# An adaLN block with a gated delta rule and a mixture of experts: the loads of x in the periods issued on ScalarE's queue instead of SyncE's

## Chip, cores and metric

The kernel runs on one core of a Trainium2 chip. The metric is the device time of one execution in microseconds (us); lower is better. A core has TensorE (PE, matmuls), VectorE (DVE), ScalarE (ACT), GpSimd (POOL) and SyncE (SP, which only issues transfers here). SP and ACT both can issue DMAs through a queue of their own. In the profile, "SPq L423" is an issue on SP's queue from line 423, and "ACTq L423" one on ACT's.

## Reference

The input x has 4 batches of 1024 tokens with 256 channels. From a condition c come six vectors for each batch: shift, scale and gate for the attention (sa, ca, ga) and for the feed-forward part (sb, cb, gb).

```python
h = _layernorm(x) * (1 + ca) + sa
x = x + ga * attention(h)
h = _layernorm(x) * (1 + cb) + sb
x = x + gb * moe(h)
```

The attention has 16 heads of 64. q, k and v are projections of h, each followed by a causal convolution over 4 tokens and a silu; k is normalised. Then a state S of 64 x 64 for each head goes from token to token:

```python
upd = vt - at[..., None] * (S @ kt)
S = clip(at * S + bt * outer(upd, kt), -5.0, 5.0)
ot = S @ qt
```

The outputs are multiplied by silu(h Wg + bg) and projected by Wo. The mixture of experts sends each token to the best 2 of 8 experts, each 256 to 512 to 256 with a gelu between, and adds the two results by their softmax weights.

## The kernel before, in words

The attention is computed in chunks of 32 tokens: one chunk is 4 batches x 32 tokens = 128 rows, and there are 32 chunks. Two neighbouring chunks make a pair; there are 16 pairs. Inside a chunk the recurrence is solved as a triangular system. `adaln_block` (L182) calls `chunks` (L362), which does the attention and the routing, and then `blocks` (L2149), which computes the experts in blocks of 256 gathered rows.

The main loop (L1505) has 16 periods. Period g runs the two state passes of pair g (stream c) and at the same time prepares pair g+1: its rows, routes, decays, keys and queries, values, triangle, rows of k and scaled keys. The order in which the steps of these streams are written is the string PLAN (L59): each letter takes one step of the stream that it names, in `work` (L1350). The letter x, twice in the string, is a step of `loads` (L1391), which loads one chunk of x; period g loads chunks 2g+6 and 2g+7, so chunks 6 to 31 are loaded in periods 0 to 12. The chunks before are loaded at the start (L446 and `later_loads`).

One chunk's load (`load_x`, L417) takes one of 9 buffers named x and issues 8 DMAs in `fill_x` (L423), 16 KB each. The rows loaded are first read in the next period, by the layer norm's statistics (L489) and by ACT (L509). Much later POOL adds the attention's result in place (L1278), SP stores the sum to x_scratch (L1280) and from there to out (L1283); then the buffer is free.

The order of the instructions on PE, DVE, ACT and POOL is the order in which the program writes them. SP's order is left to a scheduler, which places SP's issues by their dependences. The change touches L1393 alone. What the prediction follows, in the order of a period:

- L900, on SP: the decays of the pair go to g_scratch. L994, on SP: they come back spread over the partitions as sc. POOL multiplies kq by sc (L1001) and copies the last column (L1004).
- L586, on POOL: an indirect DMA sends routed rows. L1231, on POOL: aS, the decayed state, which needs L1004's result. L1196, on DVE: S = ps_s + aS.
- L920 to L956, on DVE: the triangular system, among it X (L943) and prod (L948), both with two inputs in SBUF.
- L619, on ACT: the first tap of the convolution out of PSUM for q, k (kq) and v; L628, on DVE, the other taps; L634, on ACT, silu. The projections on PE are L610, those of the gate L780 (ACT reads them in L787).
- L1149 on PE and L1154 on ACT: u, the updates of a chunk, copied out of PSUM in two halves; L1167 and L1208 on PE and L1218 on ACT: the outputs o; L1187 on PE: what u adds to the state.
- L853 on PE and L864 on ACT: kk and kk_r, the products of keys of the next pair; L1019 on PE: ps_t.
- L433 and L436, on SP: the weights w_v and w_gt; L428: w_kq. L1338, on SP: clearing of rows_scratch.

Of the kernel before, what the change touches and what calls it, by code (L numbers as in the profile page):

```python
# [361 lines left out]
def chunks(ctx, tc, a, nch, con, ones, modt, modc, x1_dram, rt, out):  # L362

    nc = tc.nc
# [18 lines left out]
    def take(pool, shape, name, tag=None, bufs=1, **more):  # L383
        tag = tag or name
        assert is_open.get(tag, 0) < bufs, tag
        is_open[tag] = is_open.get(tag, 0) + 1
        if bufs > 1:
            more["bufs"] = bufs
        return pool.tile(shape, F32, name=name, tag=tag, **more)
# [27 lines left out]
    def load_x(c, eng=nc.sync):  # L417
        x_of[c] = take(s3, [P, D], "x", bufs=9)
        fill_x(c, x_of[c], eng)

    def fill_x(c, x, eng):
        for there, here in by_batch(a["x"][c], x):
            eng.dma_start(here, there)  # L423
# [966 lines left out]

    def loads(first):  # L1391
        for c in range(first, min(first + 2, nch)):
            load_x(c)  # L1393
            yield

    def both_of(pair, prev):
# [108 lines left out]
    for g in range(npair):  # L1505

        prev, passes, bounds = both_of(now, prev)
        streams = dict(l=now.below(), c=passes, b=bounds, x=loads(2 * g + 6), z=clears())
        after, finished[:] = list(finished), []
        if g + 1 < npair:  # L1510
            x = newer
            newer = [x_of.pop(2 * g + 4 + par) for par in range(2)] if g + 2 < npair else None
            now = Pair(g + 1, x, newer, after)
            streams.update(preparing(now))
            work(streams, PLAN)
        else:

            sending = sent(after, nch - 2)
            for name in LAST:
                next(sending if name == "m" else streams[name], None)  # L1520
            work(streams, "")
# [885 lines left out]
```

## Time and profile before

| | us |
|---|---|
| three runs | 1906.1, 1913.18, 1915.0 |
| their median | 1913.18 |
| the profiled execution, its own time | 1922.9 |
| its span, from the first to the last instruction | 1921.1 |
| granted TensorE clock, mean | 0.919 |
| PE busy | 1632.0 |
| DVE busy | 1482.3 |
| ACT busy | 826.7 |
| POOL busy | 716.4 |
| one middle period (620.52 to 711.67 us): PE, DVE, ACT, POOL busy | 81.41, 75.68, 44.71, 36.88 |

The busy times are of one execution under the profiler. Issues of DMAs are not counted as busy; they are shown on rows of their own (SPq, ACTq). In a row of the timeline, the first number is the start from the beginning of the span, the second the time that it lasted, both in us; "x2" joins two neighbours of one kind; square brackets hold the idle time of the engine just before, and what ended it. The chain follows the work that ended last back from the end, at each step to what released it. An engine may have much idle time in all and yet set the end in one stage, so what follows reads one period closely.

### The profile page before, as it was taken

To read this page: it belongs to the slowest core of one execution; us is meant where nothing else is said; L and a number is where in the kernel's file an instruction comes from. 1 tells how busy PE (TensorE), PEld (TensorE's weight loads), DVE (VectorE), ACT (ScalarE), POOL (GpSimd) and SP (SyncE) were. 2 spreads that over 40 slices of the span, in tenths; PEclk is the share of its full clock that TensorE was granted. 3 is DMA by queue.
4 is the path that set the end of the run, shared out by engine and by line. 5 is a ranking of instruction groups with operands and counts; after the bars stand their busy time and mean duration, and the time that the engine had idled before them with its cause. 6 is when DMAs were issued, how large, how long until landed. Compare 5 with 4: busy or idle time off the path is not lost.

```text
span 1921.1 us, 88201 instructions
## 1 busy us (share of the span) xinstructions
PE 1632.0 (85%) x38610; PEld 1297.1 (68%) x38610; DVE 1482.3 (77%) x3622; ACT 826.7 (43%) x1652; POOL 716.4 (37%) x913
## 2 busy tenths in 40 slices
PE   5578999889989898989898989898888675989994
PEld 3456676667676766767676767676667564878883
DVE  4678797968788888878787978797968335789973
ACT  3344545444545544545445444554443112334331
POOL 1032343424342525252534343433424432454343
PEclk9889998989999998989899989998989677999997
DMA  4455444443545445354535453636343216788882
GB/s 117 127 161 129 105 108 94 107 109 95 148 115 141 123 120 137 107 134 111 146 103 150 106 153 97 161 94 153 110 112 112 56 36 207 187 208 219 231 231 35
DMA packets 431490, 249.52 MB, mean 130 GB/s; under 512 B 242996, under 2 KB 410808, under 8 KB 430840
## 3 DMA queue, kind: packets, MB, share of 16 engines
q1 hardware_dynamic: 416488, 223.65, 43.6%
q0 software_dynamic: 13664, 18.38, 5.2%
q8 instruction: 306, 5.01, 1.1%
q10 hardware_dynamic: 944, 1.77, 0.3%
q14 instruction: 88, 0.72, 0.1%
HBM read 165.99 MB, written 81.87 MB: 129 GB/s over the span
## 4 chain that ended last, share of the span: by engine, by line
PE 66%; DVE 11%; issue 7%; POOL 5%; SPq 5%; DMA 4%; ACT 3%; POOLq 0%; DVEq 0%; ACTq 0%
PE ps_q L610 22%; PE ps_hm L2116 6%; PE ps_yb L2129 6%; PE ps_w L1265 5%; PE ps_gt L780 4%; PE ps_u L1149 3%; PE ps_kk L853 3%; PE ps_o L1208 2%; PE ps_z L1127 2%; SPq L423 2%; PE ps_t L1031 2%; PE ps_s L1187 2%; DMA sc<-g_scratch 2%; PE ps_t L1019 2%; DVE kq L628 2%
## 5 line engine op out<-in xcount | busy, mean ns | idle before, releaser
L628 DVE SCALAR_TENSOR_TENSOR kq<-ps_q,w_conv,kq 128x256 f32<-128x256 f32 x768 | 319.7, 476 | 150.2 <-ACT kq L619 149.6
L610 PE MATMUL ps_q<-hT,w_kq 128*128 128x280 f32 x1024 | 323.2, 460 | 58.9 <-issue 20.6
L610 PEld LDWEIGHTS ps_q<-hT,w_kq 128*128 128x128 f32 x1024 | 203.5, 213 | 125.9 <-issue 58.2
L619 ACT ACTIVATE kq<-ps_q,w_conv 128x256 f32<-128x256 f32 x256 | 142.4, 563 | 234.8 <-PE ps_q L610 233.1
L1001 POOL TENSOR_TENSOR kq<-kq,sc 128x512 f32<-128x512 f32 x128 | 163.5, 1299 | 143.6 <-DMA sc<-g_scratch 116.5
L2136 POOL DMA_INDIRECT out<-yb,at_b x72 | 120.4, 1672 | 190.2 <-DVE gate L2106 48.7
L628 DVE SCALAR_TENSOR_TENSOR v<-ps_q,w_conv,v 128x256 f32<-128x256 f32 x384 | 158.9, 476 | 41.9 <-ACT v L619 41.7
L1231 POOL TENSOR_TENSOR aS<-S,last 128x1024 f32<-128x1024 f32 x64 | 122.5, 1914 | 135.9 <-DVE S L1196 133.4
L780 PE MATMUL ps_gt<-hT,w_gt 128*128 128x256 f32 x512 | 144.3, 410 | 29.6 <-issue 20.5
L787 ACT ACTIVATE gate<-ps_gt,b_gt 128x256 f32<-128x256 f32 x128 | 60.5, 473 | 239.3 <-PE ps_gt L780 239.1
L610 PE MATMUL ps_q<-hT,w_v 128*128 128x280 f32 x512 | 153.5, 441 | 11.6 <-issue 4.7
L2116 PE MATMUL ps_hm<-hT,w 128*128 128x256 f32 x576 | 136.4, 392 | 7.6 <-issue 5.9
L2123 ACT ACTIVATE hm<-ps_hm,b 128x256 f32<-128x256 f32 x144 | 68.2, 474 | 167.5 <-issue 120.4
L2129 PE MATMUL ps_yb<-w,hm 128*128 128x256 f32 x576 | 130.3, 379 | 0.0
L2116 PEld LDWEIGHTS ps_hm<-hT,w 128*128 128x128 f32 x576 | 112.7, 197 | 25.9 <-issue 8.9
L610 PEld LDWEIGHTS ps_q<-hT,w_v 128*128 128x128 f32 x512 | 97.7, 204 | 47.3 <-issue 13.1
L780 PEld LDWEIGHTS ps_gt<-hT,w_gt 128*128 128x128 f32 x512 | 92.0, 194 | 53.1 <-issue 28.5
L1265 PE MATMUL ps_w<-w_o,yT 128*128 128x256 f32 x512 | 121.0, 391 | 4.3 <-DVE yT L1252 2.8
L1278 POOL TENSOR_TENSOR x<-x,add 128x256 f32<-128x256 f32 x32 | 29.0, 905 | 236.4 <-DVE add L1276 232.3
L2129 PEld LDWEIGHTS ps_yb<-w,hm 128*128 128x128 f32 x576 | 106.7, 190 | 13.4 <-DVE yb L2134 0.3
L1265 PEld LDWEIGHTS ps_w<-w_o,yT 128*128 128x128 f32 x512 | 98.2, 195 | 20.1 <-DVE yT L1252 3.0
L619 ACT ACTIVATE v<-ps_q,w_conv 128x256 f32<-128x256 f32 x128 | 71.3, 573 | 93.7 <-PE ps_q L610 93.7
(265 smaller groups left out, 3230.5 us busy)
## 6 DMA issues: line engine op xcount, KB each, us to landing
w<-in_w SPq DMA_DIRECT2D x72, 512.0 KB
rows_scratch<-zero_row SPq DMA_DIRECT2D x272, 132.0 KB
w_kq<-in_w_qkv SPq DMA_DIRECT2D x260, 128.0 KB
sc<-g_scratch SPq DMA_DIRECT2D x128, 256.0 KB
w_v<-in_w_qkv SPq DMA_DIRECT2D x130, 128.0 KB
w_gt<-in_w_g SPq DMA_DIRECT2D x260, 64.0 KB
u_scratch<-u SPq DMA_DIRECT2D x128, 128.0 KB
hb<-rows_scratch SPq DMA_DIRECT2D x36, 264.0 KB
```

The source lines that it names most:

```text
L610: nc.tensor.matmul(ps.rearrange("p y t -> p (y t)"), lhsT=w[:, dc], rhs=h_t[:, dc].rearrange("p x b t -> p (x b t)"), start=(dc == 0), sto ...
L619: nc.scalar.activation(o, ps[:, :, 0:TC], AF.Identity, scale=taps[:, 0:1], bias=taps[:, KC : KC + 1])
L628: nc.vector.scalar_tensor_tensor(o, ps[:, :, j : j + TC], taps[:, j : j + 1], o, op0=ALU.mult, op1=ALU.add)
L780: nc.tensor.matmul(ps, lhsT=wg[:, dc], rhs=self.h_t[:, dc, :, :, KC - 1 :].rearrange("p x b t -> p (x b) t"), start=(dc == 0), stop=(dc == 1),
L787: nc.scalar.activation(gate[:, hp].rearrange("p x b t -> p (x b t)"), ps.rearrange("p y t -> p (y t)"), AF.Silu, bias=b_gt[:, hp : hp + 1],)
L1001: nc.gpsimd.tensor_tensor(o, o, sc[:, h4 : h4 + 4], ALU.mult)
L1231: nc.gpsimd.tensor_tensor(aS.rearrange("q b h i -> q (b h) i"), S[:, bs].rearrange("q b h i -> q (b h) i"), self.pair.last[self.par][:, bs ...
L1265: nc.tensor.matmul(ps_w, lhsT=self.yT[:, hp].rearrange("q b t -> q (b t)"), rhs=w_o[:, hp], start=(hp == 0), stop=(hp == HP - 1),)
L2116: nc.tensor.matmul(ps, lhsT=self.w1[:, dc, fc * P : (fc + 1) * P], rhs=self.hT[:, dc], start=(dc == 0), stop=(dc == 1),)
L2123: nc.scalar.activation(self.hm[:, fc], ps, AF.Gelu, bias=self.b1[:, fc : fc + 1])
L2129: nc.tensor.matmul(ps, lhsT=self.hm[:, fc, s * P : (s + 1) * P], rhs=self.w2[:, fc], start=(fc == 0), stop=(fc == 3),)
L2136: return nc.gpsimd.indirect_dma_start(out=places, out_offset=bass.IndirectOffsetOnAxis(ap=self.at[:, s : s + 1], axis=0), in_=y, in_offset ...
```

## The change

The loads of `loads` are issued on ACT's queue. The number of DMAs, their sizes and their buffers stay the same, and so does the place in the plan.

```diff
     def loads(first):
         for c in range(first, min(first + 2, nch)):
-            load_x(c)
+            load_x(c, nc.scalar)
             yield
```

`load_x(c, eng)` passes the engine on to `fill_x`, which calls `eng.dma_start` for each of the 8 parts. ACT's order is the program's, so the 8 issues stand in ACT's stream where the letter x stands in the plan: the first block of a period between L619 of a v and L1218 of an o, the second between L619 of a v and L1154, the first half of u. SP's issues of the same period are placed anew by the scheduler.

## The prediction

> **What bounds the kernel now.** I read the busy shares and the chain that ended last on the page, then the chain inside one middle period, then each engine's timeline at the two places where the change puts work.
>
> ```profile
> PE 1632.0 (85%) x38610; PEld 1297.1 (68%) x38610; DVE 1482.3 (77%) x3622; ACT 826.7 (43%) x1652; POOL 716.4 (37%) x913
> ...
> PE 66%; DVE 11%; issue 7%; POOL 5%; SPq 5%; DMA 4%; ACT 3%; POOLq 0%; DVEq 0%; ACTq 0%
> ```
>
> PE is the body of the chain. The queue of SP holds 5% of it, and line 423, the loads of x, 2% of the span (about 40 us). The chain of waits from 632 to 658 us shows where these stand; its columns are start, us, what:
>
> ```profile
> 638.78 0.59 SPq L423
> ...
> 642.91 0.43 SPq L423
> ...
> 643.92 4.59 DMA sc<-g_scratch
> ...
> 648.68 3.24 POOL kq L1001 x2
> ...
> 654.68 1.89 POOL aS L1231
> ...
> 656.59 1.22 DVE S L1196
> ```
>
> The reader is to see eight loads of x ahead of the load of sc (L994), which POOL needs for kq, then for aS, which DVE adds into the state S. But how much of it binds? DVE's timeline says:
>
> ```profile
> 656.59 1.22 DVE L1196 TENSOR_TENSOR S<-ps_s,aS 128x1024 f32<-128x1024 f32 x1 [0.92 <-POOL aS L1231]
> ```
>
> DVE was busy up to 655.66 and then waited 0.92 us. The chain follows the last releaser, so 4.6 us of issues on it are worth 0.92 us; DVE's own work comes next. Over the whole run S waits 15.4 us for aS, 10 times.
>
> I count a period from its first store to g_scratch (L900), called t0: 632.37 us here. Periods are 91.3 us long (first kk_r to first kk_r: 711.67 less 620.52 is 91.15), but two are 99.9 (339.46 to 439.38, and 1353.53 to 1453.45).
>
> **The change part by part.** Chunks 6 to 31 move: 26 blocks of 8 DMAs, two blocks in each of 13 periods. PE, DVE and POOL keep their order; ACT gets block 1 after the second v (L619) before an o (L1218), block 2 after the second v before the first u (L1154). SP's other issues are put in a new order.
>
> *Removed from SP.* From 638.78 to 643.34 is 4.56 us per period before sc, and the same again elsewhere: SP is idle before L900, from 715 to 723.9, so nothing is gained there. SP then goes from L900 over two w_v and two clearing stores (L1338) to sc: sc leaves at about t0+5.8 instead of t0+11.0. The period without loads shows this: L900 at 1365.40, sc at 1371.17, kq on POOL at 1376.19, or t0+10.8; here it is t0+16.3. Gain: at most the wait of S, 0.92 per period, 15.4 in all. The weights that now go ahead of L900 lie in SP's 8.9 idle us; if those were gone, their issue (0.55 to 0.6 each) would delay L900.
>
> *Block 1 on ACT* (in the model period at 703.7, after the v at 703.15). An issue lasts 0.42 us and the gap to the next 0.045:
>
> ```profile
> L423 SPq DMA_DIRECT2D x<-in_x x248: 310/419/2070, 1.7 to 1285.1; - x124
> L423 ACTq DMA_DIRECT2D x<-in_x x8: 317/432/608, 1.4 to 7.6; - x8
> ```
>
> Eight on ACT are 8 x 0.477 = 3.8 us. If ACT ran them strictly between its computations, the o due at 704.26 would begin at 707.5. What is queued behind: o, two kq (L619), o, hT, two silu, and then kk_r at 711.67, which had 1.45 us of idle time before it. Following that string, kq comes 1.4 us late for DVE and PE, at 13 periods 18 us. If the issues run ahead while ACT waits for PE (it idles 0.78 us before that v, 0.54 before o, 0.92 before kq), the cost is 0. No row of before shows an issue between computations, as ACT's only issues stand ahead of its first one. So 0 to 18; I take 4, nearer to nothing, since the idle times just ahead add up to 2.2 us and the loads' own waits are for transfers long landed.
>
> [...]
>
> *Block 2 on ACT.* This is the place that costs:
>
> ```profile
> 634.05 0.56 ACT L619 ACTIVATE v<-ps_q,w_conv 128x256 f32<-128x256 f32 x1 [0.38 <-PE ps_q L610]
> 635.11 0.59 ACT L1154 COPY u<-ps_u 128x512 f32<-128x512 f32 x1 [0.49 <-PE ps_u L1149]
> 636.00 0.59 ACT L1154 COPY u<-ps_u 128x512 f32<-128x512 f32 x1 [0.31 <-PE ps_u L1149]
> 641.78 0.47 ACT L787 ACTIVATE gate<-ps_gt,b_gt 128x256 f32<-128x256 f32 x1 [5.20 <-PE ps_gt L780]
> ```
>
> Eight semaphores mark the landing of all these DMAs in turn, for both queues, so each issue waits for the transfer eight before it. Block 2's loads follow directly on SP's L900, w_v and L1338 and wait for their landing. A landing takes 3.0 us by the row nearest (x_scratch stored at 693.18, read from 696.14). The second L1338 leaves at about t0+3.9 and lands at t0+6.9; the load behind it and the last one follow, so the block ends at t0+7.7 to 8.9. The first u then ends at t0+8.3 to 9.5, instead of 635.70, t0+3.3. ACT is idle for 5.20 us after the two u, so ACT has room; PE has not: ps_o (L1167) starts at 639.51, t0+7.1, in the buffer that u frees. It comes 1.2 to 2.4 us late, the first S on DVE 0.3 to 1.5 late, ps_t (L1019) as much as ps_o. Against the gain of 0.92 on the second S that leaves +0.25 to +1.45 per period, 3 to 19 in all; I take the middle, 0.8, 13 x 0.8 = 10.
>
> *What the earlier sc meets.* In each of the five periods whose sc is early today (L900 at 171.83, 264.92, 351.37, 1365.40, 1465.62), at least one two-input DVE operation next to POOL's kq is 0.9 us too long: prod (L948) takes 1.91 to 2.00 instead of 1.04. Regular periods have none. I add 0.9 for the ten that become early: 9.
>
> Sum: 10 + 4 + 9 = 23 us.
>
> **Rivals.**
>
> *Collision of POOL and DVE.* The long periods are two of those with an early sc. Timeline of POOL and then DVE in the first:
>
> ```profile
> 367.35 0.97 POOL L586 DMA_INDIRECT rows_scratch<-row_h,at  x1 [0.21 <-issue]
> ...
> 368.37 1.91 POOL L1231 TENSOR_TENSOR aS<-S,last 128x1024 f32<-128x1024 f32 x1
> ...
> 370.52 2.47 POOL L1001 TENSOR_TENSOR kq<-kq,sc 128x512 f32<-128x512 f32 x2
> ```
> ```profile
> 362.26 1.93 DVE L948 TENSOR_TENSOR prod<-T,X 128x512 f32<-128x512 f32 x1
> ...
> 368.17 4.91 DVE L943 TENSOR_TENSOR X<-X,rk 128x64 f32<-128x64 f32 x1
> ```
> ```profile
> 376.91 2.04 PE L780 MATMUL ps_gt<-hT,w_gt 128*128 128x256 f32 x4 [5.15 <-issue]
> ```
>
> X (L943) takes 0.22 us elsewhere; here it lasts until POOL's string ends, and PE idles 5.15 us behind it. The other long period has 4.92 and 5.19. With SP relieved, all ten regular periods get the order of that second one. Price per period: 5.2 (PE's idle time) to 8.6 (99.9 less 91.3), together 52 to 86. It decides if X begins at t0+16.8 to 17.1, as aS begins. Against it: the late u moves DVE too, and where X began 1.2 us after aS (period of 1465.62) it lasted only 1.09.
>
> [...]
>
> *Hidden anyway.* Both blocks run ahead in ACT's idle time, landings are quick, u is as early as needed, and an 0.9 stall cancels the gain on S: within 0.5%, 1903.6 to 1922.7.
>
> *Faster.* If L1338 lands in 1.5 us or so, u is out by t0+6.5, before PE's ps_o; then the 15.4 us of S go, and the 4.7 of the first long period with them if its alignment shifts (L943 4.91 less 0.22): -10 to -20, 1893 to 1903.
>
> *It does not do what it says:* SP could keep waiting for the same landings, as the eight semaphores are shared; then sc leaves as late as now and only ACT's cost stays, +4 to +18. I count this within the forecast.
>
> **How the numbers follow.** The profiled execution took 1922.9 us (span 1921.1 and 1.8 around it), 0.5% above the median of the runs, 1913.2. 1922.9 + 23 = 1945.9, or 1936 on the scale of the median. The forecast's own range is 1925 to 1959 (the three terms at their ends: 3 + 0 + 9 = 12, and 19 + 18 + 9 = 46). Chances: forecast 36%, collision 31% (1965 to 2000), hidden 18%, faster 15%. Faster by over 0.5% is 0.15, within 0.18, slower 0.36 + 0.31 = 0.67; 0.5% is about what a measurement of this kernel can tell from no change. The range goes from 1900 to 2000, leaving out half of the faster case and the top of the collision.
>
> **What would show it.** In the changed profile: kq (L1001) on POOL should start at t0+10.8, or up to 1.4 us later if sc waits for a landing of its own. The first u (L1154) should end at t0+8.3 to 9.5; at t0+3.3 the blocks ran ahead. The wait of S for aS should be gone. L943 near 4.9 in most periods means the collision. If the issues on ACT precede the v operations they stand behind, block 1 is free. Periods (kk_r to kk_r) should be 92 to 94 us. The forecast is wrong if ps_o on PE stays at t0+7.1, or if the periods go to 99.9 or under 91.

## The result and the profile after

The changed kernel takes 1985.6 us (median of 4 runs, 1974.3 to 1997.5) against 1913.6 before: 1.0385 times as long (95% interval 1.031 to 1.046), or +72 us. That lies inside the range on record and 50 us above the forecast. The profiled execution is the shortest of the four, 1974.3 us with a span of 1972.5, while the one of before (1922.9) was above its median; so the two profiles differ by 51 us, and the sums below are about these 51.

The page after, answering to the two lines of before:

```profile
PE 1652.5 (84%) x38610; PEld 1320.0 (67%) x38610; DVE 1501.0 (76%) x3622; ACT 821.4 (42%) x1652; POOL 718.7 (36%) x913
...
PE 65%; DVE 11%; DMA 7%; issue 7%; ACT 5%; SPq 2%; ACTq 2%; POOL 1%; POOLq 0%; DVEq 0%
```

SP's queue fell from 5% to 2% of the chain, POOL from 5% to 1%: what the change was to relieve is relieved. ACT, ACTq and DMA together went from 7% to 14%. PE does the same 38610 matmuls and is busy 20.5 us longer. This is the first hint that the same work runs slower.

The longest waits of PE that are new (us in total, times, longest; ps_l is a matmul of the routing), and what S waits for on DVE:

```profile
PE ps_l L533 <- DVE kq L628: 29.2, 14, 3.2
PE ps_o L1167 <- ACT u L1154: 28.0, 12, 4.6
```
```profile
DVE S L1196 <- PE ps_s L1187: 41.9, 14, 8.7
```

Before, ps_o did not wait for u at all, and the other waits were these:

```profile
PE ps_l L533 <- DVE kq L628: 3.5, 14, 0.2
```
```profile
DVE S L1196 <- POOL aS L1231: 15.4, 10, 2.9
DVE S L1196 <- PE ps_s L1187: 13.5, 8, 4.3
```

The 15.4 us that S waited for aS are gone altogether. Each of the two new waits of PE belongs to one block on ACT. The first block (ACT's timeline):

```profile
731.01 0.57 ACT L619 ACTIVATE v<-ps_q,w_conv 128x256 f32<-128x256 f32 x1 [0.78 <-PE ps_q L610]
731.07 4.56 ACTq L423 DMA_DIRECT2D x<-in_x  x8
735.67 0.59 ACT L1218 COPY o<-ps_o 128x512 f32<-128x512 f32 x1 [4.09 <-DMA x<-in_x]
```

The second, in a later period:

```profile
852.54 0.56 ACT L619 ACTIVATE v<-ps_q,w_conv 128x256 f32<-128x256 f32 x1 [0.38 <-PE ps_q L610]
852.55 7.27 ACTq L423 DMA_DIRECT2D x<-in_x  x8
...
859.86 1.07 ACT L1154 COPY u<-ps_u 128x512 f32<-128x512 f32 x2 [6.76 <-DMA x<-in_x]
```

The reader is to see where the issues start: 0.06 and 0.01 us after the v before them has started, and the next computation starts 0.04 us after the last issue has ended. In none of the 26 blocks does an issue start ahead of the computation written before it. The first blocks last 4.7 us on average, the second 6.6; eight issues that wait for nothing would take 3.8 by the prediction's sum.

What a late u then costs is in the chain of waits from 1137 to 1160 us (t0 is 1137.69):

```profile
1139.34 1.07 PE ps_u L1149 x64
...
1141.03 4.05 DMA rows_scratch<-zero_row
...
1145.11 0.32 ACTq L423
...
1146.88 0.59 ACT u L1154
...
1147.52 1.10 PE ps_o L1167 x68
1148.62 1.69 PE ps_gt L780 x4
```

An issue on ACT waits for the landing of one of SP's clearing stores, u waits for the issues, ps_o waits 2.32 us for u. But look at the last line: four ps_gt took 1.13 us in 14 of the 16 periods of before, this one among them, and here 1.69. The table of stretches for PE alone gives the reason (length, PE's busy time, granted clock, DMA share, GB/s):

```profile
1139.00:1144.90 5.90, 5.90 (x149) 1.00 0.38 107
1147.50:1150.00 2.50, 2.48 (x92) 0.78 0.52 157
1150.00:1152.50 2.50, 2.50 (x69) 0.50 0.85 211
1152.50:1155.00 2.50, 2.50 (x28) 0.50 0.45 111
1155.00:1157.50 2.50, 2.50 (x93) 0.50 0.62 194
1157.50:1160.00 2.50, 2.50 (x43) 0.67 0.11 30
1160.00:1165.00 5.00, 5.00 (x112) 1.00 0.22 56
```

The clock is full up to the wait and half from 1.4 us after it, for 10.2 us: 7.5 in the rows at 0.50, the rest in those at 0.78 and 0.67. PE is busy all the time. From the start of ps_o to that of S, the same stage of the same period looks like this, first before, then after:

```profile
1096.67:1102.61 5.94, 5.94 (x257) 1.00 0.24 67
```
```profile
1147.52:1155.84 8.32, 8.32 (x204) 0.58 0.61 166
```

So behind a wait of 2.3 us the same stage took 2.4 us longer, at a granted clock of 0.58 instead of 1.00.

To size this I read such stretches of 1 us over all periods (first kk_r to last kk_r, 15 periods) of every profile of this study. Idle time is 1 us less PE's busy time; time at half clock is twice (1 less the granted clock), as the clock records of the two profiles hold 1.00 and 0.50 alone. Before: 1377.5 us, 157 idle, 180 at half clock. After: 1427.5, 190 and 230. A straight line through the last 12 periods of each of the 14 profiles (168 in all; the first three of each, which fit it less well, are left out) gives length = 79.7 + 0.95 x idle + 0.33 x half-clock time, and leaves 0.7 us unexplained per period. By it, the 33 us of idle time and 50 of half clock that the change adds come to 31 + 17 = 48 of the 50.0 us: about two thirds waiting, one third clock. This is a fit and no experiment: no run changed the clock alone.

### The profile page after: what moved, and what is told of

Read it like the earlier page. It is cut to its first block, busy times and chain, and to the rows that moved or that the text cites. A ratio compares the mean times of both kernels' runs of the same rounds, so it can differ in the third digit from the quotient of the medians.

```text
span 1972.5 us, 88134 instructions
## 1 busy us (share of the span) xinstructions
PE 1652.5 (84%) x38610; PEld 1320.0 (67%) x38610; DVE 1501.0 (76%) x3622; ACT 821.4 (42%) x1652; POOL 718.7 (36%) x913
## 4 chain that ended last, share of the span: by engine, by line
PE 65%; DVE 11%; DMA 7%; issue 7%; ACT 5%; SPq 2%; ACTq 2%; POOL 1%; POOLq 0%; DVEq 0%
PE ps_q L610 19%; PE ps_hm L2116 7%; PE ps_yb L2129 6%; PE ps_gt L780 6%; PE ps_w L1265 4%; PE ps_s L1187 3%; PE ps_kk L853 3%; PE ps_o L1208 2%; PE ps_u L1149 2%; PE ps_o L1167 2%; PE ps_t L1019 2%; DVE kq L628 2%; ACTq L423 2%; DMA x<-in_x 2%; PE ps_t L1031 2%
## 5 line engine op out<-in xcount | busy, mean ns | idle before, releaser
L610 PE MATMUL ps_q<-hT,w_kq 128*128 128x280 f32 x1024 | 309.9, 444 | 49.0 <-issue 24.9
L610 PEld LDWEIGHTS ps_q<-hT,w_kq 128*128 128x128 f32 x1024 | 196.5, 205 | 113.3 <-issue 48.4
L619 ACT ACTIVATE kq<-ps_q,w_conv 128x256 f32<-128x256 f32 x256 | 141.0, 564 | 187.7 <-PE ps_q L610 186.1
L780 PE MATMUL ps_gt<-hT,w_gt 128*128 128x256 f32 x512 | 149.3, 423 | 25.3 <-issue 15.2
L610 PE MATMUL ps_q<-hT,w_v 128*128 128x280 f32 x512 | 148.6, 430 | 10.3 <-issue 4.6
L787 ACT ACTIVATE gate<-ps_gt,b_gt 128x256 f32<-128x256 f32 x128 | 60.5, 473 | 193.4 <-PE ps_gt L780 193.2
L610 PEld LDWEIGHTS ps_q<-hT,w_v 128*128 128x128 f32 x512 | 95.1, 199 | 43.2 <-issue 13.6
L2129 PEld LDWEIGHTS ps_yb<-w,hm 128*128 128x128 f32 x576 | 106.7, 190 | 13.4 <-DVE yb L2134 0.3
L2106 DVE SCALAR_TENSOR_TENSOR gate<-gates,share,gate 128x256 f32<-128x256 f32 x216 | 104.4, 483 | 7.2 <-ACT gate L2102 2.1
L1196 DVE TENSOR_TENSOR S<-ps_s,aS 128x1024 f32<-128x1024 f32 x64 | 77.4, 1209 | 41.9 <-PE ps_s L1187 41.9
```

The lines of the kernel that those rows point to most:

```text
L610: nc.tensor.matmul(ps.rearrange("p y t -> p (y t)"), lhsT=w[:, dc], rhs=h_t[:, dc].rearrange("p x b t -> p (x b t)"), start=(dc == 0), sto ...
L619: nc.scalar.activation(o, ps[:, :, 0:TC], AF.Identity, scale=taps[:, 0:1], bias=taps[:, KC : KC + 1])
L780: nc.tensor.matmul(ps, lhsT=wg[:, dc], rhs=self.h_t[:, dc, :, :, KC - 1 :].rearrange("p x b t -> p (x b) t"), start=(dc == 0), stop=(dc == 1),
L1196: nc.vector.tensor_tensor(S[:, 2 * b2 : 2 * b2 + 2], ps, aS, ALU.add)
L2106: nc.vector.scalar_tensor_tensor(self.gate[:, s], gates[:, b], self.share[:, s, b : b + 1], self.gate[:, s], op0=ALU.mult, op1=ALU.add,)
L2129: nc.tensor.matmul(ps, lhsT=self.hm[:, fc, s * P : (s + 1) * P], rhs=self.w2[:, fc], start=(fc == 0), stop=(fc == 3),)
```

## The experiments

Two theories stood against each other. A: the blocks on ACT hold up what is behind them. B: the early sc brings POOL's string into DVE's way (X, L943, lasts 4.9 us; such an X is called stuck below). Each time is a median, beside the kernel before on the same chip. The last column is read from one profiled execution of each kernel; for the kernel before it is 157 and 180, from the execution of 1922.9 us, which lies 2 to 14 us above the medians of before in this table.

| run | us | before | ratio (95%) | idle, half clock in the periods |
|---|---|---|---|---|
| changed kernel | 1985.6 | 1913.6 | 1.031 to 1.046 | 190, 230 |
| first_only | 1974.1 | 1913.8 | 1.026 to 1.039 | 185, 243 |
| second_only | 1963.7 | 1913.8 | 1.022 to 1.034 | 171, 198 |
| behind_u | 1979.0 | 1913.8 | 1.029 to 1.041 | 186, 234 |
| sp_behind_sc | 1932.5 | 1913.8 | 1.006 to 1.013 | 160, 171 |
| held_after | 2003.9 | 1908.7 | 1.042 to 1.054 | 198, 284 |
| held_before | 1911.8 | 1908.7 | 0.996 to 1.006 | 146, 172 |
| four_on_act | 1937.9 | 1908.7 | 1.007 to 1.021 | 162, 172 |
| sp_behind_all | 1925.3 | 1908.7 | 1.003 to 1.014 | 153, 163 |
| spread | 1943.0 | 1914.9 | 1.008 to 1.017 | 160, 178 |
| first_held | 1926.7 | 1914.9 | 0.999 to 1.007 | 157, 195 |
| sp_timed | 1928.1 | 1914.9 | 1.005 to 1.010 | 149, 178 |
| busy_act | 1944.1 | 1921.1 | 1.006 to 1.016 | 168, 203 |

**One block alone.** On the kernel before, even or odd chunks:

```diff
-            load_x(c)
+            load_x(c, nc.sync if c % 2 else nc.scalar)   # first_only
+            load_x(c, nc.scalar if c % 2 else nc.sync)   # second_only
```

> Only the first block of each period (even chunks) is issued on ACT, the second stays on SP. Theory A (issues stand in order between ACT's computations, and each block delays what is behind it): the wait of PE's ps_l for DVE's kq (29.2 us in the changed kernel, 3.5 in the one before) stays, the wait of ps_o for u (28.0) goes; about +20 to +30 us, 1934 to 1944. Theory B (the early sc, by the collision of POOL and DVE, makes the loss, and ACT's issues cost little): sc stays early here too, so most of the loss stays, 1960 to 1990. If ACT's issues ran ahead of its computations: within 10 us of the kernel before.

> Only the second block of each period (odd chunks) is issued on ACT, the first stays on SP. Theory A: the wait of ps_o for u stays (28 us, less the up to 15 us that S no longer waits for aS), the wait of ps_l for kq goes; about +15 to +30 us, 1928 to 1943. Theory B: sc is as early as in the changed kernel, so 1960 to 1990.

First_only: +60 us, the number of B. ps_l waits 25.3 us for kq (A's term), ps_o not at all for u, and X lasts 4.6 us or more in nine periods (4.90 at 947.94). Second_only: +50, far above A's number, but without B's mechanism: X reaches 2.6 at most in the periods with loads, u starts at t0+7.6 to 10.5, and ps_o waits 30.7 us. (This profile is the fastest of the four executions, 1946.1 us, so it accounts for less than the +50.) The two parts add to 110 where the whole is 72. So neither theory holds alone, and the costs do not add. In second_only u is late and X is not stuck in any period with loads; in first_only u is early and X is stuck in seven of them.

**The second block behind u.** The changed kernel, with the second x moved in PLAN:

```diff
-...ctcvchvvxhccctccvctstrt...
+...ctcvchvvhccctccvxctstrt...
```

> Both blocks on ACT, but the second x of the plan stands behind the two u in ACT's order, where ACT idled 5.2 us. Theory A: the first u starts at t0+2.7 again, the wait of ps_o for u goes, the first block's cost stays: 28 us less than the changed kernel's 1986, about 1950 to 1960. Theory B: the early sc is unchanged, so the time stays at 1975 to 1997, or gets worse since u no longer shifts DVE away from POOL's string (X at 4.9 in most periods).

+65 us: A's number is missed. The wait of ps_o for u is gone, but X is stuck in six periods, and ps_l still waits 29.8 us. The block, which now stands before a gate (L787), lasts beyond ACT's gap of 5.2 us:

```profile
ACT gate L787 <- DMA x<-in_x: 96.0, 12, 11.9
```

That is 8 us each. But it is not shown to cost anything: first_only, with the same first block and no second one on ACT, took +60, and the two kernels' executions overlap (1964.9 to 1980.7, and 1972.0 to 1986.1). What is left of the loss here is what first_only has too. The same kernel with sc held back was not tried.

**An early sc without ACT.** All loads on SP, the second x later in PLAN, so that SP issues sc first (two of sc, or all four):

```diff
-...vvxhccctccvctstrtccccctvrscsntcrvvcrcctcn...
+...vvhccctccvctstrtxccccctvrscsntcrvvcrcctcn...   # sp_behind_sc
+...vvhccctccvctstrtccccctvrscsntcrvvcrcxctcn...   # sp_behind_all
```

> All loads on SP as in the kernel before; only the second x of the plan is later, so that SP issues the first two loads of sc ahead of that block. Order on PE, DVE, ACT and POOL as before. Theory A: no cost on ACT, the 15.4 us that S waits for aS go: 1898 to 1913. Theory B: POOL's kq starts at t0+10.8 in every period, X lasts 4.9 us in most of them and periods take 96 to 100 us: 1965 to 2000.

> All loads on SP, the second block of a period behind the first four sc loads: sc leaves at t0+5.8 in every period, and ACT issues nothing. If the early sc alone sets off the collision: kq at t0+10.8, X at 4.9 in most periods, 1955 to 1995. If ACT's issues are needed for the loss: 1900 to 1925.

+19 and +17 us. In periods 3 to 13 (counted from 0) kq starts at t0+10.7 to 13.6, S no longer waits for aS, yet both are slower. X is stuck in three periods in each, not in most of them: where kq started at t0+12.4 or later X lasted 0.22 to 0.46 in all but one. So B's number is wrong, and so is the expectation that the relief of SP is a gain. One more stuck period than before is worth some 8.6 us, an estimate from the long periods of before (99.9 less 91.3), but in the profiles the periods add up to 1380.0 and 1372.8 us, against 1377.5 before. What is longer there stands ahead of the first kk_r (by 2.5 and 1.2 us) and behind the last (by 4.8 and 7.2). Where the 17 to 19 us come from is not settled.

**sc held back.** One dependence more: the first pair of sc waits for POOL's add into x. Held_after is the changed kernel with it, held_before the kernel before, first_held first_only.

```diff
+            done_x.append(nc.gpsimd.tensor_tensor(x1, x1, add, ALU.add))
...
+                    if w > par: yield
                     for p in range(2):
+                        one = nc.sync.dma_start(sc[...], at_heads(...))
+                        if w > par: behind(tc, one, *done_x[-1:])
```

> The changed kernel, with one more dependence: the first pair of sc loads of a period waits for POOL's add into x (L1278, ends at t0+10.5), so that POOL's kq starts at about t0+16 as it does in the kernel before. If two costs are at work, ACT's issues in order (ps_l and ps_o waiting, about 26 + 28 us) and the collision of POOL with X: the collision goes, X is 0.22 throughout, u stays late, and the time falls to 1945 to 1965. If the early sc costs nothing: 1975 to 1997 as the changed kernel. If it costs all: 1905 to 1925.

> The kernel before (all loads on SP), with the same dependence of the first sc pair on POOL's add into x. It changes little in the ten regular periods and holds sc back in the two long ones. If the collision makes those long, X falls from 4.9 to 0.22 in both and the time by 2 x 8.6 = 17 us, to 1892 to 1902. If they are long for another reason: 1906 to 1920.

> The first block alone on ACT, with the first sc pair held until POOL's add into x, so that POOL's string comes as late as in the kernel before. If the 60 us of the first block alone were its own 26 (ps_l waiting) and the rest X stuck behind POOL's string: X is 0.22 in most periods and the time 1930 to 1950. If the first block itself costs 60: 1960 to 1980.

Held_after: no stuck X (2.3 at most), and still it is the slowest of all, +95. First_held: +12, where first_only had +60. The waits of PE in held_after:

```profile
PE ps_o L1167 <- ACT u L1154: 42.4, 13, 5.1
PE ps_l L533 <- DVE kq L628: 27.1, 14, 2.9
```

and X in first_only, then in first_held (duration in ns: least, median, most):

```profile
L943 DVE TENSOR_TENSOR X<-X,rk x32: 224/226/4957, 97.0 to 1529.7; 128x64 f32<-128x64 f32 x32
```
```profile
L943 DVE TENSOR_TENSOR X<-X,rk x32: 224/225/1253, 98.6 to 1480.2; 128x64 f32<-128x64 f32 x32
```

This separates the parts. With the first block alone, holding sc takes away 48 us, and X's time above its normal 0.22 us falls from 46.8 us in all to 2.1: there the collision is the loss, and the block itself costs about 12 or less (the interval of the ratio takes in 1). With both blocks, holding sc adds 23 us, so the collision is not what the changed kernel loses by. These 23 are not the price of the late sc alone: the wait of ps_o for u also grew, from 28.0 to 42.4 us, and the time at half clock from 230 to 284. Held_before is a miss of mine. The two long periods shrank as expected, from 99.9 to 91.7 and 91.2, X never passes 0.46, and the periods of the profile add up to 1360 us instead of 1378. But the median did not move (+3). In the regular periods sc now comes later, and S waits 24.9 us for aS instead of 15.4; the stage behind the periods took 7 us longer in that profile. And the profile of before that has the two long periods is itself 14 us above the median on this chip; whether the other executions had them is not known.

**Fewer issues, or scattered ones.** Four loads of 32 rows instead of eight of 16, and eight loads in eight steps of the plan:

```diff
-        for there, here in by_batch(a["x"][c], x):
-            eng.dma_start(here, there)
+        for b in range(B):      # four_on_act
+            eng.dma_start(x[b * 32 : b * 32 + 32], a["x"][c].rearrange("(h b t) d -> b h t d", h=2, b=B)[b])
```
```diff
-            load_x(c, nc.scalar)
-            yield
+            x_of[c] = take(s3, [P, D], "x", bufs=9)      # spread; 16 letters x in PLAN
+            for o in by_batch(a["x"][c], x_of[c]): yield nc.scalar.dma_start(*o[::-1])
```

> The changed kernel with 4 loads of 32 rows for a chunk instead of 8 of 16. If the number of issues and of the landings waited for sets ACT's delay: the first u comes near t0+5, ps_o waits little, the first block costs 1 instead of 2 us; but X then meets POOL's string as in the kernel with the block behind u, so 1955 to 1975. If the delay is one landing and not eight issues: u stays at t0+7.5 to 9.4 and the time at 1970 to 1990.

> The changed kernel, but a step x of the plan issues one load instead of eight: sixteen steps at every seventh letter from the place of the first, so that ACT never has more than two issues between computations and each waits for a landing long past. If eight issues in a row between two computations are the cost: u at about t0+4, ps_l waits as little as before, and what is left is the early sc with X hit in some periods, 1915 to 1940. If every issue on ACT delays its computations wherever it stands: 1960 to 1990.

+29 and +28. With four loads the two waits of PE shrink to

```profile
PE ps_o L1167 <- ACT u L1154: 5.2, 5, 2.2
PE ps_l L533 <- DVE kq L628: 4.8, 14, 0.6
```

from 28.0 and 29.2, idle time and time at half clock return nearly to those of before, and 43 of the 72 us are gone, more than I expected. Some 7 of these are not the blocks': `fill_x` also issues the chunks loaded at the start, and the first kk_r starts at 68.1 us instead of 75.3; the periods fell from 1427.5 to 1389.0. Spread has no wait of ps_o for u and 3.5 us of ps_l, as before; 44 us are gone, and it ends 3 us above its expected range. So the bulk of the loss is eight issues in a row between two computations. The 28 us that are left are not taken apart.

**A shorter sc delay.** As sp_behind_all, with the first pair of sc behind the last L926 (a reduction on DVE) written before it:

```diff
+                done_x.append(nc.vector.tensor_reduce(T_blocks[:, :, 0:t, t], prod, AX.X, ALU.add, negate=True))
...
+                        ); behind(tc, one, *done_x[-1:][:1] if w > par else [])
```

> All loads on SP, the second block behind the first four sc loads, and the first sc pair waits for the reduction of DVE that ends at about t0+6.6 (L926), in every period: POOL's kq at t0+12 to 13.4, where X passed in the last runs. If the loss of the early sc is only where kq starts: X 0.22 in nearly all periods, S waits little for aS, 1885 to 1903. If X is hit all the same: 1910 to 1930.

+13 us, a miss. kq starts at t0+13.0 to 15.6 in periods 4 to 14 and X lasts at most 0.8 there; but then prod (L948) is hit instead (1.94 to 1.96 in five of these) and one early period still has X at 4.94. So each place of POOL's string tried without holding sc behind the add met something of DVE's solve. That this is what costs 13 us is not shown: the periods of this profile add up to 1374.5 us, 3 less than before, and the stage behind them took 10 us longer.

**Only ACT's time.** The kernel before, with ten copies at both places:

```diff
-            load_x(c)
+            load_x(c); [nc.scalar.copy(s1.tile([P, D], F32, name="spare"), w_o[:, 0]) for _ in range(10)]
```

> The kernel before, with all loads on SP, and at both places of a period ten copies of 128x256 on ACT (a copy of this size took 0.37 us, so about 3.7 us, what eight issues take without any wait); the copies go to a tile that nothing reads. sc is late as in the kernel before. If eight issues cost only the time that ACT spends on them: u ends at t0+6.6, ps_o at t0+7.1 hardly waits, ps_l waits some 25 us, 1920 to 1940. If a block of that length alone sets off what the two blocks cost with sc held (95 us): 1970 to 2010, and the waits for landings do not matter.

+23 us by the medians (ratio 1.006 to 1.016); the ten copies took 4.3 us:

```profile
735.53 4.32 ACT L1393 COPY spare<-w_o 128x256 f32<-128x256 f32 x10
...
739.76 1.06 ACT L1154 COPY u<-ps_u 128x512 f32<-128x512 f32 x2
```

u starts at t0+6.4 to 7.2 in the regular periods, ps_o follows ps_w without a wait, ps_l waits 28.1 us. A block of about the length of the issues alone, in both places, costs a third of the change. In held_after sc is late too, and it costs 95 us. What the second block has there and the copies do not is the time in which issues wait for landings (in the changed kernel 2.8 us on average, 6.6 less 3.8): it moves u past t0+7.1, where PE needs it. That these waits make the difference is argued; no run took them away and left eight issues in a row.

No version tried here is faster than the kernel before.

## Why the prediction was right or wrong

The side was right; the size of the forecast (+23) was not. A period takes 95.2 us on average, where 92 to 94 were forecast. The result lies 27 us above the forecast's own range (1925 to 1959). That the whole range, 1900 to 2000, holds it is luck: its upper part stood there for the collision, with X near 4.9 us in most periods, and in the changed kernel that happened in one of the 13 periods with loads.

*SP's relief.* Right in mechanism: kq starts at t0+9.9 to 12.3 and S waits for aS no more. The forecast 0.9 per period was not found as a gain: with ACT unchanged (sp_behind_sc, sp_behind_all) there was none, and held_after, 23 us slower without the early sc, changed the waits for u as well.

*Block 1.* "I take 4, nearer to nothing", because the issues might run ahead in ACT's idle time. They do not: all 26 blocks start 0.00 to 3.89 us behind the start of the computation before them. ps_l waits 25.7 us more than before (29.2 less 3.5), over the upper end of 18. Yet alone the block costs only 12 or so by first_held, where ps_l waits 29.7 us: part of the wait must be given back later in the period, and where is not shown.

*Block 2.* The place, the chain and the times were right: landing of L1338, issues, u, ps_o; the first u ends at t0+8.0 to 10.0 (forecast 8.3 to 9.5), and ps_o waits 2.3 us on average (28.0 in 12; forecast 1.2 to 2.4). The issues of SP and ACT name eight semaphores in turn in the trace of either kernel, each 225 or 226 times, and ACT's issue of 1145.11 waits for the one that SP's clearing store of 1141.03 marks. The price was not right. "That leaves +0.25 to +1.45 per period" is the step that failed: it let a period grow by no more than PE's wait of 1.2 to 2.4 us, less the gain on S. In periods 4 to 13 S starts 2.1 us later than before on average (t0+15.6, from 13.4), where 0.3 to 1.5 was forecast. In seven of these ten periods the matmuls between ps_o and S run at full clock, and S is 0.7 to 2.2 us late, 1.2 on average. In the other three (t0 at 556.79, 658.56 and 1137.69) the granted clock there is 0.50 to 0.58, and S is 3.7 to 4.8 us late. The clock was in no term of my sum. The fit makes it 17 of the 50 us.

*The earlier sc.* Forecast 9 us, and as a rival 52 to 86. The 9 us were for a DVE operation beside POOL's kq, read from prod: 0.9 too long in ten more periods. But prod reaches 1.92 to 1.99 in five periods of the changed kernel, as in five of the one before (1.91 to 2.00). What came is X beside POOL's aS: it adds 25.4 us over its normal length in all, 13.2 before, in stalls of 1.08 or 1.09 in eight periods, of 1.48 to 2.24 in five and of 4.6 or more in two. These 12 us are near the term, but for another operation at another place. The rival's range (1965 to 2000) holds the result, but its mechanism does not carry it: held_after has no stuck X and is slower. It does carry first_only (48 us). The reason given against it, that the late u moves DVE too, fits the changed kernel, where X began later than aS in 9 of the 13 periods.

*Faster, hidden.* Both needed a u that is in time for ps_o. In busy_act the first u ends at t0+6.9 to 7.8 and ps_o does not wait for it, and the kernel is still 23 us slower: a u in time would not have been enough while block 1 stays.

*The clock.* A wait of 2.32 us was followed by half clock for 10.2 us, and the 77 stretches at half clock within the periods of the two profiles last 3.41 us or two, three or four times as much. How long a gap has to be is not shown.

## What to carry to other kernels

Count issues as time of the engine that makes them: here eight in a row took 4.0 to 8.4 us of ACT's place in the order, the landings they waited for included. Fewer issues (four_on_act) or scattered ones (spread) gave back 43 and 44 of the 72 us; moving a whole block (behind_u) gave back 7, and with u early again X was stuck in six periods. Price a wait of PE with what the clock does afterwards: read the granted clock of the stretches just behind each wait, not the mean. And when a transfer is to come earlier, look at what its consumer then runs beside: here each earlier place of POOL's string that was tried met some part of DVE's solve.

## What the runs showed of the hardware

- In the changed kernel, issues on ACT's queue took 0.43 us each plus 0.04 between them (medians), in order with the computations: the first started 0.00 to 0.06 us after the start of the computation before it where nothing else held it (21 of 26 blocks; the other five 1.56 to 3.89, each at the landing of a clearing store, L1338), and the next computation 0.04 us after the last (0.10 in two blocks).
- Half clock after a short gap: 2.3 us idle, then half clock from 1.4 us after it, for 10.2 us (t0 at 1137.69). Not every gap does it. Of the twelve waits of ps_o for u in the changed kernel, five (2.32, 2.49, 2.60, 3.92 and 4.61 us) are followed by half clock, begun during the wait or within 1.6 us of its end and 10.2 us long; seven (2.33, two of 2.18, and 1.09 to 1.68) have none within 7 us. All twelve longer waits of ps_l (1.72 to 3.19 us) are followed by it, begun during the wait or within 2.1 us of its end, for 3.4 to 10.2 us. From 16 to 12 us before t0, behind these, the clock of the changed kernel averages 0.50 to 0.69 in periods 4 to 13, where it is 1.00 in the kernel before.
- DVE's X (0.22 us) and POOL's aS (1.9 us), in all 14 profiles: where X began 0.5 to 1.3 us after aS, it ended 0.1 us behind aS and lasted 1.1 to 1.5 us (46 cases). Where it began 0.1 to 0.6 us ahead of aS, it lasted 2.1 to 2.6 us, again to just behind aS, if POOL then paused behind a short copy (L1070) for 0.2 to 2.0 us (11 cases). If POOL's string ran on without that pause, X lasted 4.6 to 5.0 us, past the two kq behind it (32 cases). Why the order of the two starts matters so stays open.
